# One x table for each half of the columns in the first pair of a CIN kernel

## The chip, the cores and the metric

The kernel runs on one core of one Trainium2 chip. The metric is the device time of one execution in microseconds (us); less is better.

## The reference

The computation is a compressed interaction network with three layers. `X0` is the embedding `x` (1024 samples b, 39 fields f, 64 features e):

```python
def _cin_layer(Xk, X0, W, b):
    Wr = W.reshape(O, Hk, Fdim)
    return jnp.einsum('bhe,bfe,ohf->boe', Xk, X0, Wr) + b[None, :, None]
X0 = Xk = sparse_embedding
for W, b in ((W0, b0), (W1, b1), (W2, b2)):
    Xk = _cin_layer(Xk, X0, W, b)
    outs.append(Xk.sum(axis=-1))
return jnp.concatenate(outs, axis=-1) @ fc_w.T + fc_b
```

Only the sums over e leave a layer, and the last step is linear, so the kernel folds the third layer and the output weights into weights beforehand and computes the products of the first layer, all pairs of fields, in full.

## The kernel before

**Blocks and pairs.** The 1024 samples are cut into 32 blocks of 32 samples; a block has 32 x 64 = 2048 columns (`BLK`), and half of them, 1024, are `SUB`. Two blocks form a pair. A pair has a table in DRAM, `xd[k]`, of 2 x 40 rows of 2048 floats: 39 fields and a row of ones for each of its blocks. Three such tables (`NTAB`) are used in turn. The rows of x are 64 floats each, so a load of a block (`load`, L166) reads pieces of 256 bytes and writes rows that a gather can read as 8 KB.

**Tiles by gathers.** A block needs five tiles `r` of 128 rows x 2048 columns, tiles 0 to 4. Each row of a tile is one field of the block, chosen by a list (`lists`, 128 x 12 integers), and is fetched by an indirect DMA that GpSimd (POOL) issues (`gather_rows`, L173). Tiles for even blocks are in `rt[0]`, for odd blocks in `rt[1]`. Six products of two tiles (`PAIRS`: 0x1, 0x2, 3x1, 3x2, 0x4, 3x4) hold nearly all pairs of fields; VectorE (DVE) makes them (`product`, L213), and TensorE multiplies each with its weights and adds into four banks of PSUM per block (`multiply`, L556). The few pairs left over come, once per pair of blocks, from two smaller tiles `u` and `v` of 128 x 1024 (four groups of 32 rows: the two blocks and the two halves of their columns), whose product and the `u` tile itself go to TensorE in `join` (L568) in pieces of 32 rows. So a pair has 13 steps: six products and the u-v step of its even block, then six products of its odd block. A product of a block is made `AHEAD = 4` steps before TensorE uses it.

**Finish.** When a block's sums stand, ScalarE (ACT) copies one half of the rows with the output weight as a bias, DVE adds the bias b0 and multiplies (`finish`, L614), and DVE sums over e. The finish of block 0 stands on DVE after the fourth product of block 1 and ahead of its fifth.

**Order.** The order of each engine's instructions is written out by hand (`manual_schedule`); waits are semaphores. POOL's DMAs take eight semaphores in turn, and each waits for the DMA eight places before it.

**The start.** The first pair is treated differently, to begin early. Block 0's x is loaded in two halves of 16 samples by ACT's queue into two small tables `xh[0]`, `xh[1]` of 39 x 1024 (`load_half`, L251). Tiles 0 to 3 of block 0 are gathered by halves of their columns, first all from `xh[0]`, then all from `xh[1]` (L390); inside that loop, after the sixth gather, POOL issues the load of block 1 into `xd[0]`. SP's queue copies both halves from `xh` into `xd[0]` (L396), and tile 4 is gathered whole from there (L397), since it needs the row of ones that POOL wrote with `fill_ones(0)` (L371). Then follow on POOL `roll_small(0)` (u and v, L474), `roll(1)` (five whole tiles of block 1, L475), the loads of b0 and other small constants (L477 to L482), a fill of ones for `xd[2]`, and the gathers of block 2. DVE meanwhile makes, in this order, block 0's products by halves, between them the sums of weights (`weight_rows`, L516; runs of small operations, L527), then the fifth and sixth product whole, the u-v product (L221), and block 1's products.

The lists of u and v (two columns of `lists`, L473) are computed on DVE: for groups of 32 rows the table is read as rows of 1024, so that the row number is twice the field's plus the half.

Of the kernel before, what the change touches and what calls it, by code (L numbers as in the profile page):

```python
# [62 lines left out]
FT = F + 1  # L63
# [84 lines left out]
def cin_kernel(ctx: ExitStack, tc: tile.TileContext, x, w0t, b0, w1, b1, w2, b2, fc_w, fc_b, out):  # L148
# [11 lines left out]
    xd = [dram.tile([2 * FT, BLK], F32, name=f"xd{k}") for k in range(NTAB)]  # L160
    xh = [dram.tile([F, SUB], F32, name=f"xh{k}") for k in range(2)]

# [9 lines left out]

    def gather_rows(dst, table, k):  # L173
        nc.gpsimd.indirect_dma_start(  # L174
            dst, None, table, bass.IndirectOffsetOnAxis(ap=lists[:, k : k + 1], axis=0)
        )

    def roll(n, tiles=range(NT)):
# [4 lines left out]
    def roll_small(n):  # L183
        table = xd[n // 2 % NTAB].rearrange("f (t c) -> (f t) c", c=SUB)
        for k, dst in enumerate((ut, vt)):
            gather_rows(dst[n // 2 % 2], table, 2 * NT + k)

# [12 lines left out]

    lists = const.tile([128, 2 * NT + 2], I32, name="lists")
    rt = [const.tile([128, NT, BLK], F32, name=f"r{k}") for k in range(2)]
# [22 lines left out]
    with prep as prep:  # L225
# [25 lines left out]
        def load_half(k):  # L251
            nc.scalar.dma_start(
                xh[k].rearrange("f (b e) -> b f e", e=E), x[k * SB : (k + 1) * SB]
            )
# [34 lines left out]

        tmp = prep.tile([128, 16], F32, name="tmp")  # L290
        wide = prep.tile([128, 5, NT], F32, name="wide")
# [3 lines left out]
        def new():  # L295
            used[0] += 1
            return tmp[:, used[0] - 1 : used[0]]
# [70 lines left out]
        def fill_ones(k, engine, src):  # L368
            engine.dma_start(xd[k][F::FT].rearrange("r (p c) -> p r c", c=128), src)

        fill_ones(0, nc.gpsimd, ones)  # L371


        nc.vector.tensor_scalar(unit, apart, 0, None, ALU.is_equal)
        for h in (0, H):
# [3 lines left out]
            )  # L379
        r, most, seat, far = (new() for _ in range(4))  # L380
        both_of = prep.tile([128, 2], F32, name="both_of")
# [7 lines left out]
        halves = [slice(0, SUB), slice(SUB, BLK)]  # L389
        for k, cols in enumerate(halves):  # L390
            for i in range(4):
                gather_rows(rt[0][:, i, cols], xh[k], i)
                if k and i == 1:
                    load(1, nc.gpsimd)
        for k in (1, 0):
            nc.sync.dma_start(xd[0][0:F, halves[k]], xh[k])  # L396
        roll(0, (4,))  # L397

# [31 lines left out]
        fused(seat, row, 96.0, seat, ALU.is_ge, ALU.add)  # L430
        step(row, 64.0, 2.0 * FT - 1.0, far)
        nc.vector.tensor_reduce(jumps, steps_at, AX.X, ALU.add)
# [28 lines left out]
        for k, n in enumerate((8, 5)):  # L461
            for t in range(2):
# [6 lines left out]
                )  # L469
        nc.vector.tensor_tensor(seat, seat, far, ALU.add)  # L470
        nc.vector.tensor_tensor(both_of[:, 0:1], most, jumps[:, 0:1], ALU.add)
        nc.vector.tensor_tensor(both_of[:, 1:2], both_of[:, 0:1], jumps[:, 1:2], ALU.add)
        nc.vector.tensor_scalar(lists[:, 2 * NT :], both_of, 2.0, seat, ALU.mult, ALU.add)  # L473
        roll_small(0)  # L474
        roll(1)  # L475
        for h in (0, H):
# [5 lines left out]
        )  # L482
        fill_ones(2, nc.gpsimd, ones)
        w1v = w1s.rearrange("o (h f) -> o h f", f=F)
# [83 lines left out]
    def join(n, p):  # L568
        open_block(n + 1)

        def tiles(t, side):
            rows = slice(SQUARE * t, SQUARE * t + SQUARE)
            return rows, po[n + t // 2][2 * t % 4 + side]

        for side in range(2):
            for t in range(4):
                for half in range(2):
                    rows, dst = tiles(t, side)
                    at = (side + half) * H
                    nc.tensor.matmul(  # L580
                        dst[half * H : half * H + H],
                        wa[rows, NPAIR, at : at + H],
                        p[rows, bass.ts(side, MM)],
                        start=t >= 2,
                        stop=t < 2 and half == side,
                    )
        for t in range(4):
            for side in range(2):
                rows, dst = tiles(t, side)
                half = (1 - side) * H  # L590
                nc.tensor.matmul(  # L591
                    dst[half : half + H],
                    wa[rows, NPAIR + 1, H : 2 * H],
                    ut[n // 2 % 2][rows, bass.ts(side, MM)],
                    start=False,
                    stop=t < 2,
                )
# [92 lines left out]
    for at, (n, c) in enumerate(steps[:-TAIL]):  # L690
        if c == 0 and 2 <= n and n + 4 < NBLK:
            load(n + 4)
# [28 lines left out]
        if at + AHEAD < len(steps):  # L721
            n, c = steps[at + AHEAD]
            if at + AHEAD <= NPAIR:
                weight_rows(c)
            p[n, c] = product(n, c)
            if c == NPAIR - 1 and n + 2 < NBLK:
                roll(n + 2)
                if n % 2 == 0:
                    roll_small(n + 2)
                if n < 2:  # L730
                    load(n + 4, nc.gpsimd)
# [75 lines left out]
```

## Time and profile before

| | |
|---|---|
| Time, median of 3 runs | 733.65 us (732.52 to 735.16) |
| Profiled execution | 734.13 us, its span 732.1 us |
| TensorE | 723.9 us busy, 1536 matmul records of 593 ns in `multiply` |
| DVE | 638.5 us busy, of it 434.2 us in 198 products |
| POOL | 404.7 us busy, 156 gathers of r, 16 of u, 16 of v, 8 of r from `xh` |
| DMA | 197.24 MB, mean 269 GB/s |
| Granted TensorE clock | full |

The span is the time from the first to the last instruction; the time of an execution has some 2 us more. A matmul of this kernel stands twice in the trace, as two records. A gather's duration on POOL is the time to issue it; when its data has landed is told apart ("us to landing"). In the timeline a row is a group of neighbouring instructions: start, time, engine, line, operation, what it writes and reads, how many, and the idle time before it with what ended it.

### The profile page before, as it was taken

How to read it: one execution, taken by the hardware profiler on the slowest of the kernel's cores; microseconds unless marked ns; L12 is line 12 of the kernel's file. 1: busy time of each engine (PE TensorE's matmuls, PEld its weight loads, DVE VectorE, ACT ScalarE, POOL GpSimd, SP SyncE). 2: the span in 40 equal slices, each digit the busy share in tenths (PEclk: the TensorE clock that was granted, in tenths of full speed). 3: DMA queues.
4: the chain of work that ended last, by engine and by line, in shares of the span. 5: the costliest groups of instructions: out<-in, count | busy, mean ns of one | idle time of the engine just before them, and what ended most of it. 6: DMA issues, size and time to landing. Idle time of an engine off the chain costs nothing.

```text
span 732.1 us, 6359 instructions
## 1 busy us (share of the span) xinstructions
PE 723.9 (99%) x2379; PEld 314.1 (43%) x2379; DVE 638.5 (87%) x521; ACT 166.9 (23%) x240; POOL 404.7 (55%) x254
## 2 busy tenths in 40 slices
PE   8899999999999999999999999999999999999998
PEld 4344444444444444444444444444444444444443
DVE  6999799988889988889988889888898988889885
ACT  4232121222212222121221212222122221212222
POOL 6689998536555455754547555455654547545300
PEclk9999999999999999999999999999999999999999
DMA  7987889979575897757778675895767777566700
GB/s 255 374 330 285 305 322 330 359 291 347 225 283 221 288 342 279 270 226 281 279 287 320 227 294 214 305 352 236 269 249 278 301 286 267 214 259 236 287 0 0
DMA packets 65983, 197.24 MB, mean 269 GB/s; under 512 B 40110, under 2 KB 40179, under 8 KB 45984
## 3 DMA queue, kind: packets, MB, share of 16 engines
q0 software_dynamic: 28784, 185.56, 65.8%
q1 hardware_dynamic: 35468, 9.29, 5.5%
q10 hardware_dynamic: 1700, 1.99, 0.9%
q8 instruction: 18, 0.29, 0.2%
q14 instruction: 13, 0.11, 0.0%
HBM read 196.76 MB, written 10.60 MB: 283 GB/s over the span
## 4 chain that ended last, share of the span: by engine, by line
PE 95%; DVE 1%; POOL 1%; DMA 1%; issue 1%; ACT 0%; DVEq 0%
PE po L560 89%; PE po L580 4%; PE po L591 2%; DMA r<-xh,lists 1%; POOL r L174 1%; DVE p L219 0%; DVE pairs L527 0%; PE small L323 0%; POOL xd L168 0%; DVE g L610 0%; DVE sums L632 0%; ACT z L608 0%; PE tr L544 0%; POOL shifts L315 0%; DVE twice L377 0%
## 5 line engine op out<-in xcount | busy, mean ns | idle before, releaser
L560 PE MATMUL po<-p,wa 128*128 128x512 f32 x1536 | 665.4, 593 | 1.6 <-DVE p L219 1.5
L219 DVE TENSOR_TENSOR p<-r 128x2048 f32<-128x2048 f32 (+2 forms) x198 | 434.2, 2224 | 74.7 <-PE po L560 66.0
L174 POOL DMA_INDIRECT r<-xd,lists x156 | 308.7, 1979 | 259.4 <-issue 256.7
L560 PEld LDWEIGHTS po<-p,wa 128*128 128x128 f32 x1536 | 289.7, 190 | 373.2 <-issue 354.3
L608 ACT ACTIVATE z<-po,columns 64x512 f32<-64x512 f32 x128 | 87.3, 682 | 379.0 <-PE po L591 217.9
L610 DVE SCALAR_TENSOR_TENSOR g<-po,b0s,z 64x512 f32<-64x512 f32 x128 | 95.9, 749 | 9.3 <-ACT z L608 5.3
L603 ACT COPY g<-r 39x1024 f32<-39x1024 f32 x64 | 66.7, 1043 | 156.1 <-DVE sums L621 127.3
L621 DVE TENSOR_REDUCE sums<-g 103x16 f32<-103x1024 f32 x62 | 75.6, 1220 | 2.1
L174 POOL DMA_INDIRECT u<-xd,lists x16 | 38.9, 2432 | 8.4 <-issue 4.6
L174 POOL DMA_INDIRECT v<-xd,lists x16 | 39.2, 2451 | 4.9 <-issue 4.9
L580 PE MATMUL po<-p,wa 32*64 32x512 f32 x512 | 31.6, 600 | 0.0
L221 DVE TENSOR_TENSOR p<-u,v 128x1024 f32<-128x1024 f32 x16 | 19.5, 1219 | 0.0
L580 PEld LDWEIGHTS po<-p,wa 32*64 32x64 f32 x512 | 9.4, 131 | 20.2 <-issue 20.2
L591 PE MATMUL po<-u,wa 32*64 32x512 f32 x256 | 17.0, 587 | 0.0
L174 POOL DMA_INDIRECT r<-xh,lists x8 | 7.9, 989 | 5.3 <-DVE blocks L425 3.2
L591 PEld LDWEIGHTS po<-u,wa 32*64 32x64 f32 x256 | 5.7, 132 | 8.0 <-issue 8.0
L545 ACT COPY wa<-tr 128x128 f32<-128x128 f32 x8 | 2.1, 266 | 18.3 <-PE tr L544 18.3
L527 DVE TENSOR_TENSOR pairs<-both 128x2 f32<-128x2 f32 (+27 forms) x59 | 6.1, 173 | 0.3
L279 PE MATMUL idle<-const-float32-1.0 128*128 128x256 f32 (+2 forms) x12 | 5.4, 555 | 0.8 <-PEq L794 0.8
L544 PE MATMUL tr<-unit,pairs 128*128 128x128 f32 x8 | 2.3, 286 | 1.4 <-DVE pairs L527 1.4
L279 PEld LDWEIGHTS idle<-const-float32-1.0 128*128 128x128 f32 x12 | 2.6, 254 | 2.4 <-issue 2.2
L544 PEld LDWEIGHTS tr<-unit,pairs 128*128 128x128 f32 x8 | 1.1, 139 | 5.3 <-issue 1.7
(97 smaller groups left out, 54.2 us busy)
## 6 DMA issues: line engine op xcount, KB each, us to landing
xd<-in_x SPq DMA_DIRECT2D x28, 312.0 KB
r<-xd,lists POOLq DMA_INDIRECT x156, 9.1
xd<-in_x POOLq DMA_DIRECT2D x3, 312.0 KB, 7.6
w2s<-in_w ACTq DMA_DIRECT2D x1, 624.0 KB
w1s<-in_w ACTq DMA_DIRECT2D x1, 624.0 KB
w0s<-in_w0t ACTq DMA_DIRECT2D x1, 380.2 KB
xh<-in_x ACTq DMA_DIRECT2D x2, 156.0 KB
xd<-xh SPq DMA_DIRECT2D x2, 156.0 KB
```

What stands on the lines that cost most here:

```text
L174: nc.gpsimd.indirect_dma_start(dst, None, table, bass.IndirectOffsetOnAxis(ap=lists[:, k : k + 1], axis=0))
L219: nc.vector.tensor_tensor(p[:, cols], r[:, i, cols], r[:, k, cols], ALU.mult)
L221: nc.vector.tensor_tensor(p[:, 0:SUB], ut[n // 2 % 2], vt[n // 2 % 2], ALU.mult)
L279: nc.tensor.matmul(idle[:, 0:cols], nc.const_aps.tensor(1.0, (128, 128), F32), nc.const_aps.tensor(1.0, (128, cols), F32), start=True, sto ...
L527: nc.vector.tensor_tensor(out, diagonal(a, b, sa, sb), diagonal(b, a, sb, sa), ALU.add)
L560: nc.tensor.matmul(po[n][m], wa[:, c, side : side + 2 * H], p[:, bass.ts(m, MM)], start=n % 2 == 0 and c == 0, stop=n % 2 == 1 and c == NP ...
L580: nc.tensor.matmul(dst[half * H : half * H + H], wa[rows, NPAIR, at : at + H], p[rows, bass.ts(side, MM)], start=t >= 2, stop=t < 2 and ha ...
L591: nc.tensor.matmul(dst[half : half + H], wa[rows, NPAIR + 1, H : 2 * H], ut[n // 2 % 2][rows, bass.ts(side, MM)], start=False, stop=t < 2,)
L603: nc.scalar.copy(gt[H : H + F], rt[n % 2][0:F, 0, bass.ts(m, SUB)])
L608: nc.scalar.activation(z[one], po[n][m][other], AF.Identity, bias=fc0s[other])
L610: return lambda: nc.vector.scalar_tensor_tensor(g[n][m // 2][0:H, at], po[n][m][one], b0s[one], z[one], ALU.add, ALU.mult)
L621: nc.vector.tensor_reduce(sums[:, b_at : b_at + SB], g[n][m // 2].rearrange("p (b e) -> p b e", e=E), AX.X, ALU.add,)
```

## The change

Each half of the first pair's columns now has a table of its own, `xh[k]`, of 2 x 40 rows of 1024: the fields of block 0 and a row of ones, then the same for block 1.

- POOL fills the two rows of ones of each `xh` before the first gather (two small DMAs in place of one); `xd[0]`'s own ones are filled later, behind the fill for `xd[2]`.
- The copies from `xh` to `xd[0]` on SP are gone. Block 1's x is loaded into the lower half of `xh[0]` and `xh[1]` by two DMAs of POOL, which now stand behind all eight half gathers of block 0's tiles 0 to 3 and ahead of tile 4.
- Tile 4 of block 0 and all five tiles of block 1 are gathered by halves, so ten gathers in place of five for block 1. `u` and `v` of the first pair take two gathers each, of 64 rows.
- The groups of 32 rows of u and v now run over the halves first and the blocks second, for all pairs: two more list columns, a changed formula on DVE (two more small operations), and in `join` the bank of a group changes accordingly.
- Blocks 6 and 7 are loaded by POOL's queue (`n < 4`) and no longer by SP's.

```diff
-    xh = [dram.tile([F, SUB], F32, name=f"xh{k}") for k in range(2)]
+    xh = [dram.tile([2 * FT, SUB], F32, name=f"xh{k}") for k in range(2)]
...
     def gather_rows(dst, table, k):
+        at = lists[0 : dst.shape[0], k : k + 1]
         nc.gpsimd.indirect_dma_start(
-            dst, None, table, bass.IndirectOffsetOnAxis(ap=lists[:, k : k + 1], axis=0)
-        )
+            dst, None, table, bass.IndirectOffsetOnAxis(ap=at, axis=0)
+        )
+
+    def roll_half(n, i, h):
+        k = n * NT + i
+        rows = F if n == 0 and i < NT - 1 else (n + 1) * FT
+        gather_rows(rt[n][:, i, bass.ts(h, SUB)], xh[h][0:rows], k)
...
     def roll_small(n):
-        table = xd[n // 2 % NTAB].rearrange("f (t c) -> (f t) c", c=SUB)
         for k, dst in enumerate((ut, vt)):
-            gather_rows(dst[n // 2 % 2], table, 2 * NT + k)
+            if n:
+                table = xd[n // 2 % NTAB].rearrange("f (t c) -> (f t) c", c=SUB)
+                gather_rows(dst[n // 2 % 2], table, 2 * NT + k)
+            else:
+                for h in range(2):
+                    gather_rows(dst[0][h * H : h * H + H], xh[h], 2 * NT + 2 + k)
...
-        fill_ones(0, nc.gpsimd, ones)
-
+        for k in range(2):
+            nc.gpsimd.dma_start(
+                xh[k][F::FT].rearrange("r (p c) -> p r c", c=128), ones[0:8]
+            )
...
-        for k, cols in enumerate(halves):
-            for i in range(4):
-                gather_rows(rt[0][:, i, cols], xh[k], i)
-                if k and i == 1:
-                    load(1, nc.gpsimd)
-        for k in (1, 0):
-            nc.sync.dma_start(xd[0][0:F, halves[k]], xh[k])
-        roll(0, (4,))
+        for at in range(8):
+            roll_half(0, at % 4, at // 4)
+        for k in range(2):
+            nc.gpsimd.dma_start(
+                xh[k][FT : FT + F].rearrange("f (b e) -> f b e", e=E),
+                xv[:, BB + k * SB : BB + (k + 1) * SB, :],
+            )
+        for k in range(2):
+            roll_half(0, 4, k)
...
-        step(row, 64.0, 2.0 * FT - 1.0, far)
+        step(row, 64.0, 1.0 - 2.0 * FT, far)
...
-        nc.vector.tensor_tensor(seat, seat, far, ALU.add)
+        nc.vector.tensor_scalar(half_seat, seat, float(FT), None, ALU.mult)
+        fused(seat, seat, 2.0 * FT, far, ALU.mult, ALU.add)
...
-        nc.vector.tensor_scalar(lists[:, 2 * NT :], both_of, 2.0, seat, ALU.mult, ALU.add)
+        nc.vector.tensor_scalar(lists[:, 2 * NT + 2 :], both_of, half_seat, None, ALU.add)
+        nc.vector.tensor_scalar(
+            lists[:, 2 * NT : 2 * NT + 2], both_of, 2.0, seat, ALU.mult, ALU.add
+        )
         roll_small(0)
-        roll(1)
+        for i in range(NT):
+            for k in range(2):
+                roll_half(1, i, k)
...
-        fill_ones(2, nc.gpsimd, ones)
+        for k in (2, 0):
+            fill_ones(k, nc.gpsimd, ones)
...
-            return rows, po[n + t // 2][2 * t % 4 + side]
+            return rows, po[n + t % 2][t // 2 * 2 + side]
...
-                        start=t >= 2,
-                        stop=t < 2 and half == side,
+                        start=t % 2 == 1,
+                        stop=t % 2 == 0 and half == side,
...
-                    stop=t < 2,
+                    stop=t % 2 == 0,
...
-        if c == 0 and 2 <= n and n + 4 < NBLK:
+        if c == 0 and 4 <= n and n + 4 < NBLK:
             load(n + 4)
...
-                if n < 2:
+                if n < 4:
                     load(n + 4, nc.gpsimd)
```

More of the change, by code (lines that the diff above doesn't have):

```diff
@@ L199, in cin_kernel @@
     kfin = const.tile([NY * 32, 1], F32, name="kfin")
-    lists = const.tile([128, 2 * NT + 2], I32, name="lists")
+    lists = const.tile([128, 2 * NT + 4], I32, name="lists")
     rt = [const.tile([128, NT, BLK], F32, name=f"r{k}") for k in range(2)]
@@ L252, in load_half @@
             nc.scalar.dma_start(
-                xh[k].rearrange("f (b e) -> b f e", e=E), x[k * SB : (k + 1) * SB]
+                xh[k][0:F].rearrange("f (b e) -> b f e", e=E), x[k * SB : (k + 1) * SB]
             )
@@ L287, in cin_kernel @@
         spin()
-        tmp = prep.tile([128, 16], F32, name="tmp")
+        tmp = prep.tile([128, 18], F32, name="tmp")
         wide = prep.tile([128, 5, NT], F32, name="wide")
@@ L379, in cin_kernel @@
             )
-        r, most, seat, far = (new() for _ in range(4))
+        r, most, seat, far, half_seat = (new() for _ in range(5))
         both_of = prep.tile([128, 2], F32, name="both_of")
```

## The prediction, made before the changed kernel had run

> **What bounds the kernel now.** I read the page's busy times first, then the chain in order of time, then POOL's and DVE's timelines beside each other for the first 70 us.
>
> ```profile
> PE 723.9 (99%) x2379; PEld 314.1 (43%) x2379; DVE 638.5 (87%) x521; ACT 166.9 (23%) x240; POOL 404.7 (55%) x254
> ```
>
> TensorE is busy for 99% of the span. The chain says where it is not:
>
> ```profile
> 17.88 7.80 DMA r<-xh,lists
> ...
> 25.70 1.22 DVE p L219
> 26.92 0.98 DVE pairs L527 x11
> ...
> 30.94 0.33 PE tr L544
> 31.27 3.44 PE po L560 x8
> ```
>
> From 31 us on the chain is matmuls only, so the change can win only ahead of that, and can lose only by opening a gap after it. Ahead of it the chain hangs on the eighth half gather (tile 3, second half): issued at 17.88, landed at 25.67, and 5.27 us of DVE work later (25.67 to 30.94) TensorE runs on without a stop. Call that landing L.
>
> Now the two timelines, POOL's and then DVE's (start, us, engine, line):
>
> ```profile
> 24.30 0.94 POOL L174 DMA_INDIRECT u<-xd,lists  x1 [3.77 <-DVE p L219]
> 25.54 0.94 POOL L174 DMA_INDIRECT v<-xd,lists  x1 [0.30 <-issue]
> ...
> 28.04 3.09 POOL L174 DMA_INDIRECT r<-xd,lists  x1 [0.30 <-issue]
> 31.43 2.60 POOL L174 DMA_INDIRECT r<-xd,lists  x1 [0.30 <-issue]
> 34.34 2.70 POOL L174 DMA_INDIRECT r<-xd,lists  x1 [0.30 <-issue]
> 37.35 3.54 POOL L174 DMA_INDIRECT r<-xd,lists  x1 [0.30 <-issue]
> 40.89 1.16 POOL L477 DMA_DIRECT2D b0s<-in_b  x2
> ...
> 53.02 12.45 POOL L174 DMA_INDIRECT u<-xd,lists  x1 [0.30 <-issue]
> ```
>
> ```profile
> 27.82 2.35 DVE L219 TENSOR_TENSOR p<-r 128x1024 f32<-128x1024 f32 x2
> 30.09 0.79 DVE L527 TENSOR_TENSOR pairs<-both 128x22 f32<-128x22 f32 x7
> 30.80 2.28 DVE L219 TENSOR_TENSOR p<-r 128x2048 f32<-128x2048 f32 x1
> 33.01 1.00 DVE L527 TENSOR_TENSOR pairs<-both 128x22 f32<-128x22 f32 x10
> 33.93 2.27 DVE L219 TENSOR_TENSOR p<-r 128x2048 f32<-128x2048 f32 x1
> 36.13 0.61 DVE L527 TENSOR_TENSOR pairs<-both 128x9 f32<-128x9 f32 x7
> 36.66 1.21 DVE L221 TENSOR_TENSOR p<-u,v 128x1024 f32<-128x1024 f32 x1
> ...
> 53.57 13.37 DVE L219 TENSOR_TENSOR p<-r 128x2048 f32<-128x2048 f32 x6
> ```
>
> A gather's issue takes 0.94 us, but one that meets a product of DVE takes 2.6 to 3.5, and at 53.02 it takes 12.45 beside six products in a row. The ends fit one rule: the gathers of 28.04, 31.43 and 34.34 end 1.04, 1.02 and 0.91 us after the next run of small weight sums starts (30.09, 33.01, 36.13). So a gather gets through in a break between products, one to a break, while the plain DMAs at 40.89 pass beside a product at 0.58 each.
>
> [...]
>
> **The change, part by part.** Steps of block 0 are c0 to c5 (pair products) and c6 (u times v); a and b are a tile's halves.
>
> *Removed ahead of L.* Block 1's load stood in POOL's queue between the sixth and seventh half gather; landings there (issue plus the tile view's time to landing) are 22.05 for tile 1b (14.03 + 8.0), 23.15 for the load (14.96 + 8.2) and 24.40 for tile 2b (16.34 + 8.1), so it costs 1.1 us of the queue. The two copies (2 x 156 KB) cost 0.8 us at about 400 GB/s, and at most 2.0, which is what the landings of tiles 2a and 3a lie late (4.9 us from tile 1a, 9.06 + 5.5, to tile 3a, 11.55 + 7.9, where a gather's step is 1.25 to 1.5 elsewhere). So L moves by 1.9, at most 3.1: from 25.67 to 23.8, at best 22.6. I take 1.87 and shift DVE's chain by it: small sums start at 24.97, 28.22, 31.14 and 34.26, c6 could start at 34.79, and TensorE reaches the join at 39.11 (from 40.98). TensorE's idle time between its first product matmul (15.49) and 30.94 is about 4 us, of which DVE's order lets some 2.6 go at most. Alone this would be -1.9 us.
>
> *Free.* Two more small DVE operations (0.07 to 0.2 us each) lie in the 0.92 us that DVE waits before 10.91. The second fill of ones (0.7) lies in POOL's 3.2 us of idle time before 7.71. The SP copies leave a queue that waits anyway. Loads 6 and 7 go from SP to POOL, a block and more ahead of use, at 1.06 us each on an engine that is 55% busy. The join writes the same number of matmuls to four banks as before; no price.
>
> *Added: four gathers for u and v, ten for block 1's tiles in place of five, all behind a later load.* The loads are now issued at about 17.5 and 18.3 and land behind tile 3b. The first u gather waits for the first load: 23.8 + 0.55 (half of 1.1) = 24.35, and from landing to issue it was 1.15 us (23.15 to 24.30), so 25.45. That is inside the small sums from 24.97; from there one gather per break:
> - u, first half: 25.45 to 26.39.
> - u, second half: meets c3; ends 28.22 + 1.04 = 29.26.
> - v, first half: meets c4; ends 31.14 + 1.02 = 32.16.
> - v, second half: meets c5; ends 34.26 + 0.91 = 35.17.
>
> Landing follows the end of the issue by 3.6 us when the queue is short (the v gather of 65.78: 1.97 + 3.6 = 5.5): 38.8. DVE stands at c6 from 34.87 until then, c6 ends at 40.05, and the join starts 1.0 late, block 1 could start at 42.85.
> - Block 1's tiles 0a, 0b, 1a now get through at 1.24 us apiece (35.47 to 38.89), 1b meets c6 and ends 40.05 + 0.8 = 40.86. The first half gather of 512 KB lands 4.3 us after its issue ends (5.4 from its start at 7.71, less 1.05) and I take 4.0 here: 44.85. First product of block 1: 44.9 to 47.2. TensorE starts block 1 at 47.2, 3.4 us later than 43.81.
> - Tiles 2a to 3a end at 44.6; 3b meets that product and ends at 48.0, 4a meets the next and ends at 50.5, 4b at 51.75. Tile 3b lands at 52.0, so the third product runs 52.05 to 54.35 (TensorE wants it at 54.1), the fourth to 56.55.
> - b0 is queued behind all ten: issued at 51.75 and 52.3, and at 4.8 us to landing (the ones fill of 43.63) there at 57.1. The finish of block 0 needs it, and took 5.5 us (48.06 to 53.57): to 62.6. The fifth product of block 1 stands behind it on DVE: to 64.9. TensorE wants it at 61.3 (four steps of 3.45 us, and 0.3 of wait) and gets it at 64.9.
>
> Before, the fifth step began at 43.81 + 4 x 3.45 = 57.6. So the loss is 64.9 - 57.6 = 7.3 us. Behind it DVE's 2.2 us products catch up on TensorE's 3.45 us steps before block 2, and the next gathers have slack: I see no third stop.
>
> Unknown costs. If L is 22.6 all of this comes 1.2 us earlier: +6.1. A 64-row gather may be cheaper than the 0.94 us; between nothing saved and all four free of blocking it is worth 0 to 4 us. Landing may take 3.3 to 5.6 us (the v gather of 25.54 took 6.6, its issue in that): -0.7 to +2. I take +7.0.
>
> **The sum.** The profiled execution took 734.13 us, its span 732.1 with 2.0 around it; the median of the runs is 733.65, so I add the same 7.0 to it: 740.65, span about 739.1.
>
> **Rivals.**
> - *The gathers pass.* If 64-row gathers, or half gathers that read a shorter list, slip between products, block 1 is there in time and only the shorter start is left: 733.65 - 1.9 = 731.8, at best -2.6: 731.0. For it: at 44.56 a gather got past a pair of products after 2.26 us, and the two gathers at 24.30 and 25.54 met products and lost nothing. Against it: those two fell into waits of DVE for data; the four after them all lost 1.7 to 2.6 us. It decides from the point at which u and v are issued by 30 us.
> - *Half blocked.* One product boundary lets a gather through, so v is out one break earlier (its issue ends near 32). Then c6 waits until about 36, block 1 starts some 1 us late, and the finish still waits for b0, which makes the fifth product about 5 us late: 738.5. With a DVE that catches up before the fifth product it is the 3.4 us of block 1's start, or less: 736.5.
> - *It does not pay at all*, the DMA queues being full from 17 to 44 us: then L stays and nothing else moves, 733.6. [...]
>
> **How the numbers follow.** Likeliest is the blocked case, 0.68: its own range is 738.5 to 743. Half blocked 0.14 (736 to 738.5). Passing, or not paying, 0.18 (731 to 734). From 736.0 to 743.0 about 0.8 is held. Less than 0.3% (2.2 us) can hardly be told from no change here; of the 0.18 a bit more than half lies beyond it. Faster 0.10, same 0.08, slower 0.82.
>
> **What would show it.** Right: the u and v issues after the first take 2.5 us or more; DVE has a gap of 3 to 4 us before c6 ended by a v landing; TensorE has gaps before block 1 and before its fifth step, the second about as long as the first; b0 lands near 57. L near 23.8 and the transpose at 30.94 near 29.1 show the first step. Wrong: v issued by 30 us, or no gap in TensorE after 31 us.

## The result, and the profile after

The changed kernel takes 741.09 us (median of 6 runs, 738.73 to 742.54); the kernel before took 733.68 us beside it (6 runs, 732.52 to 735.16). The ratio is 1.0096, with a 95% interval of 1.0077 to 1.0116: 0.96% slower. The profiled execution took 740.87 us, its span 739.1 us (before: 734.13 and 732.1). So 7.0 us of span are to be found.

The profile's busy times show where they went, in part: TensorE is busy for 728.0 us (723.9 before) with the same 2379 matmul records, so some of them took longer, and the other 2.9 us are waits. POOL has 6.6 us more (404.7 before), DVE is the same (638.5 before):

```profile
PE 728.0 (98%) x2379; PEld 315.6 (43%) x2379; DVE 638.9 (86%) x523; ACT 167.1 (23%) x240; POOL 411.3 (56%) x267
```

TensorE's own timeline has the two stops (start, us, engine, line, what; in square brackets the wait ahead of the row and what ended it):

```profile
28.77 0.33 PE L564 MATMUL tr<-unit,pairs 128*128 128x128 f32 x1
...
40.62 1.98 PE L600 MATMUL po<-p,wa 32*64 32x512 f32 x32 [1.74 <-DVE p L231]
...
47.52 17.04 PE L580 MATMUL po<-p,wa 128*128 128x512 f32 x33 [2.76 <-DVE p L229]
```

The transpose at 28.77 stood at 30.94 before: the start is 2.2 us shorter, as the change meant. TensorE could have started the join near 38.9 and block 1 near 41.6. It starts block 1 at 47.52, where the kernel before started it at 43.81: 3.7 us later, with the shorter start already spent.

The chain of waits (start, us, engine and line) then shows block 1 itself taking longer. First the kernel before, then the changed one:

```profile
43.81 41.40 PE po L560 x96
...
87.97 41.40 PE po L560 x96
```

```profile
47.52 44.08 PE po L580 x96
91.60 1.90 PE po L600 x32
93.50 0.86 PE po L611 x16
94.36 41.40 PE po L580 x96
```

The same 96 matmuls took 41.40 us in every block before; here block 1 takes 44.08. The next block starts at 94.36 (87.97 before). Together 3.71 + 2.68 = 6.4 us; 0.35 us more is in one later join (1.21 us at 137.66, where others take 0.86), the rest in the tail. Why 44.08 is told by the table by stage (stretch; length; busy us of TensorE, weight load, DVE, ACT and POOL; granted clock; DMA share; GB/s):

```profile
32.00:34.00 2.00, 2.00 (x7) 1.01 (x6) 2.00 (x1) 0.95 (x8) 1.86 (x1) 1.00 0.49 133
34.00:36.00 2.00, 2.00 (x6) 0.80 (x5) 0.70 (x8) 0.83 (x4) 1.70 (x2) 1.00 0.17 29
...
46.00:48.00 2.00, 0.47 (x1) 0.48 (x2) 1.73 (x2) 0.58 (x1) 2.00 (x1) 0.50 1.04 424
...
50.00:52.00 2.00, 2.00 (x4) 0.72 (x3) 1.78 (x2) 0.23 (x1) 2.00 (x4) 0.50 0.57 166
52.00:54.00 2.00, 2.00 (x5) 0.87 (x4) 2.00 (x2) 0.00 (x0) 2.00 (x5) 0.80 0.61 211
```

From 46 to about 52.8 us the granted clock is 0.50: after its wait TensorE works at half speed for about 5.3 us and loses half of that. The first two rows show what went before the wait: from 32 to 36 us the DMA engines run nearly empty (133 and 29 GB/s), at a time when the kernel before moved 407 and 410:

```profile
32.00:34.00 2.00, 2.00 (x6) 0.92 (x5) 2.00 (x12) 0.00 (x0) 2.00 (x1) 1.00 1.01 407
34.00:36.00 2.00, 2.00 (x7) 0.88 (x6) 2.00 (x2) 0.95 (x8) 1.70 (x2) 1.00 1.06 410
```

They are nearly empty because hardly anything is issued. POOL's timeline of the changed kernel:

```profile
24.75 0.92 POOL L175 DMA_INDIRECT u<-xh,lists  x1 [1.52 <-DVE p L229]
25.97 2.95 POOL L175 DMA_INDIRECT u<-xh,lists  x1 [0.30 <-issue]
29.22 2.61 POOL L175 DMA_INDIRECT v<-xh,lists  x1 [0.30 <-issue]
32.14 2.81 POOL L175 DMA_INDIRECT v<-xh,lists  x1 [0.31 <-issue]
35.26 0.95 POOL L175 DMA_INDIRECT r<-xh,lists  x1 [0.30 <-issue]
...
39.01 0.94 POOL L175 DMA_INDIRECT r<-xh,lists  x1 [0.30 <-issue]
...
48.59 2.27 POOL L175 DMA_INDIRECT r<-xh,lists  x1 [0.31 <-issue]
50.85 1.17 POOL L496 DMA_DIRECT2D b0s<-in_b  x2
```

Three gathers in a row take 2.6 to 2.95 us and not 0.94. They end at 28.92, 31.83 and 34.95. DVE's runs of small weight sums begin at 27.92, 30.98 and 34.07, so each gather ends 0.85 to 1.0 us after a break between products began. The first gather of block 1 is issued at 35.26, the one that completes tile 1 (the second half) at 39.01 to 39.95; in the kernel before, tiles 0 and 1 were out by 31.13. DVE shows what waits for them:

```profile
34.07 0.63 DVE L547 TENSOR_TENSOR pairs<-both 128x9 f32<-128x9 f32 x7
39.34 1.22 DVE L231 TENSOR_TENSOR p<-u,v 128x1024 f32<-128x1024 f32 x1 [4.63 <-PE po L580]
45.18 2.29 DVE L229 TENSOR_TENSOR p<-r 128x2048 f32<-128x2048 f32 x1 [4.62 <-DMA r<-xh,lists]
...
55.28 1.53 DVE L630 SCALAR_TENSOR_TENSOR g<-po,b0s,z 64x512 f32<-64x512 f32 x2 [0.53 <-issue]
```

The wait of 4.63 us is put down to TensorE; but the product's second input is `v`, whose last gather was out at 34.95. That `v` came last is read from the kernel with filler matmuls below, which has nearly the same times there and names it:

```profile
39.41 1.23 DVE L231 TENSOR_TENSOR p<-u,v 128x1024 f32<-128x1024 f32 x1 [4.76 <-DMA v<-xh,lists]
```

The 4.62 us ahead of 45.18 are the landing of tile 1.

### The profile page after: what moved, and what is told of

Its sections match the earlier page's. It is cut to its first block, busy times and chain, and to the rows that moved or that the text cites. A ratio compares the mean times of both kernels' runs of the same rounds, so it can differ in the third digit from the quotient of the medians.

```text
span 739.1 us, 6371 instructions
## 1 busy us (share of the span) xinstructions
PE 728.0 (98%) x2379; PEld 315.6 (43%) x2379; DVE 638.9 (86%) x523; ACT 167.1 (23%) x240; POOL 411.3 (56%) x267
## 4 chain that ended last, share of the span: by engine, by line
PE 93%; POOL 2%; DMA 2%; DVE 2%; issue 1%; ACT 0%; DVEq 0%
PE po L580 87%; PE po L600 4%; PE po L611 2%; DMA r<-xh,lists 2%; POOL r L175 1%; DVE p L229 1%; POOL v L175 1%; POOL u L175 1%; PE small L333 0%; DVE g L630 0%; DVE sums L652 0%; ACT z L628 0%; POOL shifts L325 0%; DVE twice L389 0%; DVE blocks L438 0%
## 5 line engine op out<-in xcount | busy, mean ns | idle before, releaser
L229 DVE TENSOR_TENSOR p<-r 128x2048 f32<-128x2048 f32 (+2 forms) x198 | 434.2, 2225 | 75.8 <-PE po L580 64.9
L175 POOL DMA_INDIRECT u<-xd,lists x15 | 26.9, 1792 | 4.6 <-issue 4.0
L175 POOL DMA_INDIRECT v<-xd,lists x15 | 26.5, 1769 | 4.6 <-issue 4.6
L175 POOL DMA_INDIRECT r<-xh,lists x20 | 24.1, 1207 | 8.1 <-issue 5.8
L611 PE MATMUL po<-u,wa 32*64 32x512 f32 x256 | 18.5, 587 | 0.2 <-issue 0.2
L175 POOL DMA_INDIRECT v<-xh,lists x2 | 5.4, 2714 | 0.6 <-issue 0.6
L175 POOL DMA_INDIRECT u<-xh,lists x2 | 3.9, 1934 | 1.8 <-DVE p L229 1.5
L168 POOL DMA_DIRECT2D xd<-in_x x4 | 4.2, 1054 | 0.0
```

The costliest lines, as they stand in the source:

```text
L175: nc.gpsimd.indirect_dma_start(dst, None, table, bass.IndirectOffsetOnAxis(ap=at, axis=0))
L229: nc.vector.tensor_tensor(p[:, cols], r[:, i, cols], r[:, k, cols], ALU.mult)
L611: nc.tensor.matmul(dst[half : half + H], wa[rows, NPAIR + 1, H : 2 * H], ut[n // 2 % 2][rows, bass.ts(side, MM)], start=False, stop=t % 2 ...
```

## The experiments

The theory: a gather cannot be issued while DVE makes products; whatever puts POOL's queue later than the break ahead of c3 (block 0's fourth product, whose two halves are made in a row) costs a break, about 3 us, for each gather behind it. The rivals that were set against it: the late load alone, the number of gathers alone, the half clock alone, and DMA bandwidth. All ratios below are to the kernel before, in runs beside it; the changed kernel has 1.0096.

### Breaks in the products

To the changed kernel, three tiny writes of DVE between the halves of c3, and c4 and c5 cut in halves with such writes between:

```diff
+    def rest():
+        for _ in range(3):
+            nc.vector.memset(pause, 0.0)
...
     p[n, c] = product(n, c, halves[0])
+    rest()
     product(n, c, halves[1], p[n, c])
...
-            p[n, c] = product(n, c)
+            if at + AHEAD < NPAIR:
+                p[n, c] = product(n, c, halves[0])
+                rest()
+                product(n, c, halves[1], p[n, c])
+            else:
+                p[n, c] = product(n, c)
```

> The changed kernel, with three tiny DVE writes put between the halves of the fourth product of block 0, and its fifth and sixth product cut into halves with three such writes between. Blocked issue (gathers get through only between products): three more openings, so the second u gather and both v gathers take about 1.2 us each instead of 2.6 to 2.9, v is issued by 31 us, the first product of block 1 ends near 44.4 instead of 47.5, the clock's dip at 46 us is gone or shorter: about 735.5 (734 to 738). Late load, or full DMA queues: nothing changes in the waits, 741 to 742.

Measured: 737.54 us, 1.0059 (1.0038 to 1.008). The same edit to the kernel before, as a control:

> The kernel before with the same writes and halves. Blocked issue: the four gathers of block 1 that took 2.6 to 3.5 us to issue get shorter, but TensorE had no gap there, so the time stays: 733.7, at most 0.5 more from DVE's extra 0.3 us before the transpose at 30.9. If the openings helped by anything else than the gathers' issue, this kernel would get faster too.

Measured: 733.47 us, 1.0001 (0.999 to 1.0012). In the kernel before, where TensorE doesn't wait for block 1's gathers, the time stayed. In the changed kernel, where it does, the same rests take back half of the loss. In POOL's timeline of the first of the two kernels both v gathers go out in 1.1 and 1.5 us, and block 1's first gather at 30.76 in place of 35.26:

```profile
27.55 1.09 POOL L175 DMA_INDIRECT v<-xh,lists  x1 [0.31 <-issue]
28.95 1.51 POOL L175 DMA_INDIRECT v<-xh,lists  x1 [0.30 <-issue]
30.76 1.15 POOL L175 DMA_INDIRECT r<-xh,lists  x1 [0.31 <-issue]
```

Without the rests the two v gathers took 2.61 and 2.81 us; three writes of 0.1 us were enough. But TensorE still waited for block 1:

```profile
44.67 43.16 PE L580 MATMUL po<-p,wa 128*128 128x512 f32 x96 [3.19 <-issue]
```

Tile 1 landed at 42.2, 5 us after its issue, with the DMA engines nearly full (busy share 0.93 and 0.89 in the two stretches from 38 to 42 us). So these rests remove half of the loss; what is left in this kernel is the landing of tile 1 and, behind it, a shorter stretch of half clock (granted clock 0.52 and 0.63 in the two stretches from 46 to 50 us).

### The half clock

To the changed kernel, two matmuls with zero weights ahead of the first join and three behind it, so that TensorE isn't idle:

```diff
+            if not n:
+                keep_warm(po[n][0], 2)
             join(n, p.pop((n, c)))
+            if not n:
+                keep_warm(po[n + 1][0], 3)
```

> The changed kernel with matmuls by zero weights in TensorE's two waits of the first pair: two ahead of the join, three behind it (each 0.86 us), which add zero to a bank. If the half clock from 46.0 to 52.8 us follows from TensorE's idle time, it goes; TensorE then reaches the fifth product of block 1 near 61.3 and waits for it until 63.1, so only 0.9 us of the 2.6 come back: about 740.2. If the fifth product isn't late, all 2.6: 738.4. If the clock drops for another reason: 741.1 with the dip still there.

Measured: 741.18 us, 1.0104 (1.0082 to 1.0126): no gain. The clock stayed full (1.00 in every stretch from 38 to 68 us), and TensorE's timeline shows what took its place:

```profile
46.15 2.85 PE L675 MATMUL po<-const-float32-1.0,const-float32-0.0 128*128 128x512 f32 x6
48.84 13.89 PE L580 MATMUL po<-p,wa 128*128 128x512 f32 x32
63.29 7.13 PE L580 MATMUL po<-p,wa 128*128 128x512 f32 x16 [0.56 <-DVE p L229]
```

The last filler ends at 48.8, so block 1 starts 1.3 us later than in the changed kernel, and its fifth product isn't ready before 63.3. In the changed kernel TensorE came to that product at 63.96, and the product was ready at 63.08. The half clock therefore costs at most 0.9 us net there: behind it stands the fifth product, nearly as late. This kernel shows one thing more. Its POOL held other gathers than the changed kernel's (the second half of tile 4 for 5.25 us, the first of u for 2.88 us), and still issued block 1's first gather at 35.21, against 35.26: what counts is the number of openings, not which gather meets them.

### Load, gathers of u and v, halves: one at a time

Undo the late load: both loads of block 1 behind the sixth half gather, where the kernel before has its one.

```diff
         for at in range(8):
             roll_half(0, at % 4, at // 4)
-        for k in range(2):
-            nc.gpsimd.dma_start(
-                xh[k][FT : FT + F].rearrange("f (b e) -> f b e", e=E),
-                xv[:, BB + k * SB : BB + (k + 1) * SB, :],
-            )
+            if at != 5:
+                continue
+            for k in range(2):
+                nc.gpsimd.dma_start(
+                    xh[k][FT : FT + F].rearrange("f (b e) -> f b e", e=E),
+                    xv[:, BB + k * SB : BB + (k + 1) * SB, :],
+                )
```

> The changed kernel with block 1's two loads issued after the sixth half gather, where the kernel before has its load. Late load as the cause: the u gather isn't late any more and the loss goes, 733 to 735. Blocked issue: u starts about 1 us earlier and v gets out one break earlier (near 32), but the eight gathers that the first product of block 1 needs still share the same few breaks, so it is ready only some 0.5 to 1.5 us earlier: about 740 (738.5 to 741).

Measured: 740.93 us, 1.0109 (1.0081 to 1.0137). Nothing gained. u's gathers go out without delay, but there are two of them, and the third gather meets c3; the one that completes tile 1 ends at 39.88, where the changed kernel had 39.95:

```profile
25.89 1.15 POOL L175 DMA_INDIRECT u<-xh,lists  x1 [0.30 <-issue]
27.34 3.09 POOL L175 DMA_INDIRECT v<-xh,lists  x1 [0.30 <-issue]
```

The late load alone, in the kernel before:

```diff
-                if k and i == 1:
-                    load(1, nc.gpsimd)
+        load(1, nc.gpsimd)
         for k in (1, 0):
             nc.sync.dma_start(xd[0][0:F, halves[k]], xh[k])
```

> The kernel before with one part of the change alone: block 1's x loaded behind the eighth half gather and not between the sixth and seventh; copies, whole gathers and u and v in one gather each stay. Held-up issue: L comes 1.1 us sooner, but u, which waits for the load, is issued near 27 us, inside c3: u ends near 30, v 33, tile 0 36, tile 1 38.3; it lands near 43.3, TensorE starts block 1 at about 45.6 and not 43.8: 735.5 us, 734.5 to 737. Rival, the place of the load is no matter, the halves are all of the loss: 732.5, the 1.1 us of L gained.

Measured: 737.9 us, 1.0049 (1.0035 to 1.0064). With whole tiles, single gathers of u and v and the copies all kept, the load's place alone makes half of the loss. POOL, then DVE and TensorE of this kernel:

```profile
26.06 3.26 POOL L174 DMA_INDIRECT u<-xd,lists  x1 [6.07 <-DVE p L219]
29.63 2.60 POOL L174 DMA_INDIRECT v<-xd,lists  x1 [0.30 <-issue]
32.54 2.70 POOL L174 DMA_INDIRECT r<-xd,lists  x1 [0.30 <-issue]
35.54 1.97 POOL L174 DMA_INDIRECT r<-xd,lists  x1 [0.30 <-issue]
```

```profile
26.01 2.35 DVE L219 TENSOR_TENSOR p<-r 128x1024 f32<-128x1024 f32 x2
...
43.15 2.29 DVE L219 TENSOR_TENSOR p<-r 128x2048 f32<-128x2048 f32 x1 [6.46 <-DMA r<-xd,lists]
```

```profile
45.50 43.16 PE L559 MATMUL po<-p,wa 128*128 128x512 f32 x96 [3.46 <-DVE p L219]
```

u is issued at 26.06, 0.05 us after c3's products have begun at 26.01; in the kernel before it went at 24.30. Block 1 starts at 45.50 (45.6 was expected). The time is 2.4 us over the expectation of 735.5. Two losses were not counted in it: the block runs 43.16 us and not 41.40 for the half clock (granted clock 0.70, 0.50 and 0.95 in the three stretches from 46 to 52 us), and TensorE waits another 1.57 us in the next block. They can't be set against the 2.4 us one for one, since the profiled execution, at 740.03 us, was the longest of its twelve.

One gather each for u and v: both halves in one table of four parts, block 1's ten half gathers kept. The edit also needs ten more list columns and a few more small DVE operations, which are not shown here:

```diff
-    xh = [dram.tile([2 * FT, SUB], F32, name=f"xh{k}") for k in range(2)]
+    xh = dram.tile([4 * FT, SUB], F32, name="xh")
...
-                for h in range(2):
-                    gather_rows(dst[0][h * H : h * H + H], xh[h], 2 * NT + 2 + k)
+                gather_rows(dst[0], xh, 2 * NT + 2 + k)
```

> The changed kernel with one edit: both halves lie in one DRAM table of four parts (160 x 1024: block 0 left and right, block 1 left and right), so u and v are one gather of 128 rows each and not two of 64; everything else, block 1's ten half gathers too, stays. Held-up issue: two issues fewer stand in the queue while the products c3 to c5 run. u at about 24.8, v gets c3's break (28.9), tiles 0a and 0b those of c4 and c5 (31.8, 35.0), 1b is issued by 37.5 and not 39.95 us; v lands by 33 and c6 no longer waits; the first product of block 1 starts near 42.7 and not 45.2, b0 and the fifth product come 2.5 us sooner too: 738.5 us, 737 to 739.5. Rival, DMA-bound: with the whole gathers of block 1 (another edit) tile 1 was issued 1.2 us sooner and landed no sooner, since 2 MB took 7 us; then the edit brings at most 1 us: 740 to 741.5.

Measured: 737.48 us, 1.0047 (1.0032 to 1.0061), 3.6 us below the changed kernel and inside the 737 to 739.5 expected of two issues fewer. It has the late load and one gather each for u and v, as the kernel with the late load alone has, and comes to the same time (1.0047 and 1.0049), half tiles or whole. Its profiled execution was one of the slower of its runs (span 737.1) and doesn't show the expected path to the end: v was out at 30.3 and c6 no longer waited, but tile 1 went at 38.31 to 39.25 and TensorE still waited 4.02 us ahead of block 1.

Block 1's tiles whole, from a table of their own that a third load fills, u and v in halves:

```diff
+        nc.gpsimd.dma_start(
+            x1[0:F].rearrange("f (b e) -> f b e", e=E), xv[:, BB : 2 * BB, :]
+        )
         for k in range(2):
             roll_half(0, 4, k)
...
-            for k in range(2):
-                roll_half(1, i, k)
+            gather_rows(rt[1][:, i], x1, i)
```

> The changed kernel with one edit: block 1's x goes into a DRAM table of its own with whole rows (40 x 2048), so its five tiles are gathered whole, 5 gathers of 8 KB rows and not 10 of 4 KB rows; block 0 stays in halves. Held-up issue, my theory: the first of these gathers still is issued at about 35.3 us, behind the small tiles, but tiles 0 and 1 are then both issued by 37.5 us, against 40.0 us in the changed kernel; they land by about 43.0, the first product of block 1 ends at 45.3 against 47.5, TensorE waits about 3.7 us and not 5.9, and b0 is issued 6 us earlier, so finish(0) and the fifth product no longer limit: about 737 us, 735.5 to 738.5. Rival, the count of the gathers is no matter because only the hold of the small tiles counts: within 0.3% of the changed kernel, 739 to 743. Rival, the halves of block 0 are the whole cost: also no change.

Measured: 740.1 us, 1.0084 (1.0071 to 1.0096). The expectation failed: five issues fewer brought 1 us. In the profiled execution, the longest of its six, tile 1 was out only 1.2 us earlier (38.73 against 39.95), as block 1's first gather went 1.3 us later than in the changed kernel (36.52), and it landed no earlier:

```profile
37.78 0.95 POOL L177 DMA_INDIRECT r<-x,lists  x1 [0.30 <-issue]
45.77 2.29 DVE L231 TENSOR_TENSOR p<-r 128x2048 f32<-128x2048 f32 x1 [5.30 <-DMA r<-x,lists]
```

How many gathers there are behind u and v is thus of little weight. Tile 1 landed 7 us after the end of its issue, while the DMA engines moved 268 to 352 GB/s from 38 to 44 us with a busy share of 0.87 to 0.98; why not more isn't shown.

So the load's place and the split of u and v are two causes, and each costs time without the other. Undoing the load alone brings nothing, since the split is still there; the load alone, without the split, costs half of the loss, and undoing the split alone leaves that half.

### All causes taken back, and the rests

Whole tiles and rests together (here the first rest stood ahead of the second halves of c0 to c2, and c3 was not broken):

> Both edits together: whole gathers for block 1, and three tiny VectorE writes between the halves of the products c3, c4 and c5 of block 0. With rests alone TensorE still waited from 41.5 to 44.7 us although the gather of tile 1b was issued by 36.6: it landed at 42.2, because from 24 to 44 us the DMA engines were full at some 300 GB/s (4 KB rows at 200 to 220 ns each), where the kernel before moves 400 with its 8 KB rows (310 to 325 ns each). If it is row size and hold-up together: v lands at 34.9 as with rests alone, tiles 0 and 1 then need 16 rows of 315 ns on each DMA engine, 5.0 us, and land by 40.0; first product to 42.3 or 42.5; TensorE's wait is under 1 us, no half clock, block 1 starts at 42.4 against 43.8 in the kernel before: 732.3 us, 731.5 to 733.5, so at or just below the kernel before. Rival, the row size is no matter (only the hold-up): no better than with rests alone, 736 to 738.5. Rival, the half clock comes after any wait at the join: 734 to 735.5.

Measured: 737.39 us, 1.0044 (1.0023 to 1.0065). The expectation failed again, and the time is that of the rests alone (737.54), which is the range of the rival, for which whole tiles add nothing. The rests stood elsewhere, though, so the two are no clean pair. In the profile TensorE started block 1 at 43.51, with full clock (1.00), 1.1 us after the time expected; it also waited 0.90 us for the fifth product of block 1 and 1.82 us for that of block 2, which were not expected. The 16 runs go from 734.36 to 741.74 us, so that one profile stands for them poorly.

With one gather each for u and v as well, rests in c3 to c5, and the third load behind tile 4's gathers:

> The changed kernel with three edits: u and v one gather each from one table, block 1's tiles whole from a table of their own (its load is last of the three), and three tiny VectorE writes between the halves of c3, c4 and c5. Held-up issue: v is out by 26 us, tiles 0 and 1 by 31 us; both have landed by 38 to 39, the first product ends by 41.3 and TensorE goes from the join (ends near 41.5) to block 1 with no wait and no half clock; the start that the change shortened by 2.2 us is then kept, less the 0.7 us that the rests and the third load cost: 732.3 us, 731.3 to 733.5, at or below the kernel before. Rival, DMA-bound: gathers that are issued in a row land slowly, tile 1 at 40 us, TensorE waits 1 to 2 us, and the fifth product of block 1 waits again: 734 to 737.

Measured: 739.31 us, 1.0068 (1.0044 to 1.0093): worse, and 7 us above the expectation, through the place of the third load. It stood in POOL's queue behind a gather that a row of four products held up, and tile 0 waited for it:

```profile
21.02 5.26 POOL L176 DMA_INDIRECT r<-xh,lists  x1 [0.30 <-issue]
...
34.54 1.25 POOL L176 DMA_INDIRECT r<-x,lists  x1 [3.10 <-DMA x<-in_x]
```

That is the hold-up once more, in another place. Two last ways of putting it right. First, no rests; the loads of the small tables early, u and v one gather each, whole tiles:

> The changed kernel with its three costs taken back and the rest kept (the halves of block 0 gathered from tables that the loads fill, no copies): block 1's x loaded behind the sixth half gather, u and v one gather each from one table, block 1's tiles whole from a table of their own, whose load stands behind the eighth half gather. No rests. Held-up issue: the gathers meet the same breaks as in the kernel before: u near 24.7, v near 25.9, tile 0 takes c3's break (30.4), tile 1 is out by 32 us and lands near 38 to 39; no wait of TensorE at the join, no half clock: 733.5 us, 732 to 735, the same as before within 0.3%; the early load takes back the shorter start. Rival, a cost that none of these edits touches (the join's banks, the 4 KB rows of block 0, the third load): above 736.

Measured: 736.88 us, 1.0053 (1.0034 to 1.0071); above the expectation, and where the rival had it, a cost that none of these edits touches. In the profiled execution (735.04 us, the shortest of its six) TensorE didn't wait at the join, and waited 1.29 us at the fifth product. v had still met c3 (27.04, 3.08 us). With the load's place, the split and the half tiles of block 1 all taken back, 3.1 of the 7.4 us are still lost; what the longer runs lose was not recorded and stays open.

Second, the load left late as in the change, the third load ahead of tile 4, and one rest more ahead of the second halves of c0 to c2:

> As the kernel with all three edits, with two things put right: the third load stands ahead of tile 4's gathers (there it stood behind a gather that was held up for 5.3 us and landed at 34, so that tile 0 waited 3.1 us for it), and one more rest ahead of the second halves of c0 to c2, for tile 4's second half. Block 1's x stays late. Held-up issue: tile 4 is out by 22.8, u and v by 25.5, tile 1 by 29 us; tile 1 lands by 39.5, TensorE waits less than 0.5 us after the join: 732.5 to 734, and below the kernel before only if block 2's fifth product, for which TensorE waited 1.8 us with whole gathers and rests, is in time. Rival, the DMA engines are full from 22 us on at under 300 GB/s and tile 1 lands at 41 whatever the issue: no better than with whole gathers and rests, 736 to 738.

Measured: 734.4 us (22 runs), 1.0004 (0.9992 to 1.0016): the whole loss is gone, though the time is just above what was expected, 732.5 to 734. POOL issues v at 25.30 and tile 1 by 29.6, the DMA engines are full from 14 to 42 us (busy share 0.97 to 1.07), and TensorE goes from the join to block 1 without a wait:

```profile
40.49 14.00 PE L584 MATMUL po<-p,wa 128*128 128x512 f32 x32
55.64 27.73 PE L584 MATMUL po<-p,wa 128*128 128x512 f32 x64 [1.15 <-DVE p L229]
...
86.07 14.00 PE L584 MATMUL po<-p,wa 128*128 128x512 f32 x32
101.50 27.73 PE L584 MATMUL po<-p,wa 128*128 128x512 f32 x64 [1.44 <-DVE p L229]
```

Block 1 starts 3.3 us ahead of the kernel before, and the lead is given back: 1.15 and 1.44 us at the fifth products of blocks 1 and 2, the rest at smaller stops. The first four products come as their tiles land, at 420 to 430 GB/s, and the fifth starts at 53.30, where the kernel before had it at 53.57. One last edit put every finish one product later, behind that fifth product:

```diff
-        if at - 1 in over:
-            finish(over[at - 1])
-            fields(over[at - 1] + 1)
+        if at - 2 in over:
+            finish(over[at - 2])
+            fields(over[at - 2] + 1)
```

> The kernel with rests, one gather each for u and v, whole tiles of block 1 and the third load ahead of tile 4, with one more edit: every block's finish (and the copies for the next block) comes one product later, behind the fifth product of the next block and not ahead of it. In that kernel TensorE started block 1 at 40.5 us, 3.3 us ahead of the kernel before, and gave 1.15 us back at the fifth product of block 1 and 1.44 us at that of block 2, each time with the 5.5 us of the finish ahead of that product on VectorE. If the place of the finish is what gives the gain back: the fifth product ends near 50 us where TensorE wants it at 54.5, both waits go, and with them 2.6 us: 731.8 us, 731 to 733, faster than the kernel before by 0.2 to 0.4%. Rival: the finish then closes an opening that the gathers of the next block used, and the wait comes back at the first product of a later block: 734 or more.

Measured: 734.06 us, 0.9997 (0.9986 to 1.0008). In its profile both waits are gone and blocks 1 and 2 run at 41.47 and 41.81 us, with a span of 730.6; but 731.8 us was expected, and over 14 runs the kernel can't be told from the one before. No version was measurably faster than the kernel before.

## Why the prediction was right

741.09 us against 740.65 predicted, inside the range of 736 to 743. The blocked case that was taken for the likeliest came, and by its path up to block 1's start. Behind that one of its terms was mis-sized, and a loss that it didn't have filled the gap; that the sum agrees to within 0.5 us is luck.

- **The start.** Predicted 1.87 us shorter, at most 3.1; the transpose of 30.94 came at 28.77, 2.17 us. The size is right. The chain no longer hangs on the eighth half gather, though, but on the sixth (issued at 13.91, landed at 20.98); DVE then makes the halves that remain without a gap.
- **What was free.** The lists, fills and moved loads show no wait on the chain. The join's changed bank order wasn't tried by itself.
- **One gather per break.** The ends of u's second and v's two gathers were predicted at 29.26, 32.16 and 35.17, and were 28.92, 31.83 and 34.95. c6 was to end at 40.05 and ended at 40.56; the join was to be 1.0 us late and was 1.74, since v took 4.4 us from the end of its issue to the start of c6 and not 3.6.
- **Block 1's start.** Predicted 47.2, was 47.52, by two errors that cancel. The gather that completes tile 1 was to be held up by c6 to 40.86; it passed just ahead of it and ended at 39.95. Its landing was to take 4.0 us and took 5.2. So this number too is in part luck.
- **The second stop** is the step that was mis-sized. The fifth product of block 1 was to be ready at 64.9, 3.6 us late. It was ready at 63.08 (60.80 and 2.28 us). The finish before it began at 55.28 and not at 57.1, after a wait of 0.53 us that the trace puts down to no other engine and to no DMA; the missing input was probably b0, issued at 51.4, 0.9 us earlier than predicted. At full clock TensorE would have come at 61.3 (47.52 and four steps of 3.45 us), so the stop would have been 1.8 us.
- **The half clock** is the loss that the prediction didn't have. TensorE came to the fifth product at 63.96, behind the half clock, and did not stop. The half clock came after a wait of 2.76 us (with one of 1.74 us ahead of the join), and in the kernel with breaks after a single one of 3.19 us. The prediction's own sum had 4.35 us between the join's end (42.85) and block 1 (47.2), with no price on it; the kernel before, where TensorE waits at most 1.3 us for a product, shows no half clock (granted clock 1.00). The kernel with filler matmuls shows that the two losses cover each other: without the half clock the fifth product still isn't ready before 63.3.
- **The sum.** Predicted +7.0; the span has +7.0, made of 3.7 (block 1 late), 2.7 (half clock, with the second stop hidden in it) and 0.6 behind it. The predicted 7.0 was taken from a sum of 7.3: 3.4 for block 1's start, 3.6 for the second stop and 0.3 of wait between the two.
- **The rivals.** That the gathers pass is refuted by the three issues of 2.6 us and more; that they are half blocked, by the end of v's issue at 34.95, where that rival had it near 32. Half blocked is what the kernels with one gather less each, or with only the late load, came to: 737.5 to 737.9, in the range given for it (736 to 738.5). That nothing moves is refuted by the start.

What isn't settled: why gathers land slowly in some stretches. In the kernel with breaks the DMA engines were nearly full from 24 to 42 us (busy share 0.96 on average) at some 290 GB/s; in the one with whole tiles, single gathers and more rests they moved 414 to 430 from 30 to 42. The changed kernel's own half gathers reach 412 to 424 from 44 to 48 us, so the shorter rows alone are not the reason.

## What to carry to other kernels

Read a queue that is held up by another engine by its openings: count the instructions that have to pass before the last one that matters, and ask which opening each gets; u, issued 0.05 us after c3 had begun, took 3.26 us and not 0.94. Two causes that lead through the same opening don't add up, so undoing one of them may show nothing; do one alone in the kernel before as well. When a change makes a stop of TensorE as long as those here (2.76 to 4.02 us; one of 2.99 us brought no half clock), put the half clock in the sum (1.5 to 2.7 us here), and look for the stop that stands behind it.

## What the runs showed of the hardware

- The half clock lasted 3.4 us in four kernels (breaks, one gather each, late load alone, whole tiles) and 6.8 us, twice that, in two (the changed kernel and the early load). This is reckoned for the first pair from the granted clock in stretches of 2 us: what a stretch lacks of 1.00, times its length, times two, since a stretch that is low throughout reads 0.50 (0.52 and 0.63 from 46 to 50 us in the kernel with breaks give 3.4). It cost block 1's 96 matmuls (41.40 to 41.47 us at full clock) 1.5 to 1.8 us in the first four and 2.6 to 2.7 us in the other two. It can begin after the matmuls have gone on: in the kernel with breaks they went on at 44.67, the clock was still 1.00 from 44 to 46 us, and by the 0.52 it fell at about 46.1.
- The length of a wait alone doesn't tell whether it comes. It came after waits of 3.19, 3.46, 3.72, 3.93 and 4.02 us, and in the changed kernel after 2.76 us, with 1.74 us ahead of the join; after one of 2.99 us (the kernel whose third load was late) the clock stayed full (1.00 in every stretch from 14 to 54 us):

```profile
46.27 14.00 PE L584 MATMUL po<-p,wa 128*128 128x512 f32 x32 [2.99 <-DVE p L229]
```

- A gather that meets products which follow each other without a gap may wait for all of them: 9.53 us from 60.96 in the changed kernel beside four products, and 14.1 to 14.7 us in ten of the others, in the kernel with breaks beside six. Three tiny writes of DVE, 0.1 us each, between two products were opening enough: with them the two v gathers took 1.09 and 1.51 us, without them 2.61 and 2.81.
- DMA engines that had run nearly empty did not land a gather later than full ones: in the kernel with whole tiles (busy share 0.34 to 0.49 from 32 to 38 us, 0.87 to 0.98 from 38 to 44) tile 1 of block 1 landed at most 8.0 us after its issue began (37.78 to 45.77), in the kernel before (1.01 to 1.08 from 28 to 38 us) 9.5 us after.
